# Two tiles to a transpose, the split behind it, and the update's first layer as one product in a graph network kernel

## The chip, the cores and the metric

The kernel runs on one core of a Trainium2 chip. A core has five engines that run side by side, each through its own instructions in order: TensorE (PE, with its weight loads listed as PEld), VectorE (DVE), ScalarE (ACT), GpSimd (POOL) and SyncE (SP), which here issues most DMAs. TensorE writes to PSUM, of which a bank holds 128 partitions of 512 float32. The metric is device time in microseconds (us); the median of nine runs before the change is 902.21 us (900.59 to 903.66).

## The reference: what is computed

There are 6250 nodes with 64 features and 206250 directed edges (100000 random pairs both ways, and a loop for each node), sorted by destination. Cut to what matters:

```python
h = max(layernorm(x), 0)
# first network: two graph convolutions
g = relu(relu((h + sum_of_neighbours(h)) @ W1 + b1) @ W2 + b2)
x = x + relu((g + sum_of_neighbours(g)) @ W3 + b3) @ W4 + b4
# second network: messages, their sum, update
h = max(layernorm(x), 0)
y = mlp3(h; WM1, WM2, WM3)                 # 64 -> 128 -> 128 -> 64, relu between
z = segment_sum(y[src], dst)
out = x + mlp3(concat([h, z]); WU1, WU2, WU3)   # 128 -> 128 -> 128 -> 64
```

All of it is float32. The sum over neighbours is taken as a product with a dense matrix of edge counts.

## The kernel before

**Tiles and layouts.** The nodes are 49 tiles of 128 (`NT`). "By node" is a tile with nodes on the partitions and features along the row; "by feature" has features on the partitions and up to four tiles of nodes (512 columns) along the row. The layers (`layer`, L444) want by feature, and a last layer (`last`, L453) gives by node back, one small product per tile.

**Precision.** Plain float32 products (FP) and float32r products (FR) are both used. A float32r operand is exact enough when the value is split into a rounded half and the rest (`halves`, L251: ACT copies with rounding, DVE subtracts). The product then runs over both halves.

**Build (to about 380 us).** For each of the 49 tiles a strip of the count matrix A is built from the edge list by one-hot products (L419), written to DRAM by SP (L425), and used at once for the first convolution (L569). Layers of that convolution run between, group by group. The halves of three weights are taken when the second strip is done (L611, L612): `w1p`, `m1p` and `u1p`. All weights are loaded at the start by SP's queue, ahead of the first store of A. A weight made with `twice` (L120) is loaded into both halves of the partitions, by two DMAs.

**Two sweeps (`sweep`, L693).** Each goes over 13 groups of up to four destination tiles (`GROUPS`: eleven of 4, one of 3, one of 2). A group takes 13 pieces of up to four source tiles. For a piece, SP loads counts as bytes (five buffers `a`), ACT or DVE widens them to float32r (L710, six buffers `ar`; pieces 1, 3, 6, 8 and 11 are ACT's), and TensorE multiplies into the group's sum `acc` (L717, two banks). The first sweep has two products per source tile (both halves of `h2r`), the second has one: its stationary operand is 64 columns of the rounded half of y beside 64 of the rest, so the sum of messages comes as two parts, on partitions 0 to 63 and 64 to 127.

**Behind each group** come the layers, `conv2` (L664) in the first sweep and `conv3` (L680) in the second. They are written one group late, behind the end of the next group's sum. A scheduler then places each instruction in its engine's queue, so the layers' products stand among the sweep's. The last groups of the first sweep reach into the second, which therefore leaves the last two pieces of its first two groups to the end of these.

`conv2` takes the group's sum through W3 and W4 (`ps_y` from w4), adds to x (`xs`), normalises to `h` (`norm`, L225), and calls `by_feature` (L438): `vr` gets both halves of h side by side, each tile is turned by its own transpose over 128 columns (L432, into bank `tf`), and ACT copies the bank to `h3f` (L435), which now holds the rounded half on partitions 0 to 63 and the rest on 64 to 127. Two products with `m1p` (the halves of the doubled WM1) give the message's first layer, one with `m2` the second, four small ones with `m3` the last; the result is split into `yr`.

`conv3` copies the sum to `f2` (`plain`, L659), and makes the update's first layer of three products into one bank: two float32r ones of `h3f` (kept for all nodes) with `u1p`, and a float32 one of `f2` with `u1z`, which holds the lower half of WU1 twice and so adds the sum's two parts:

```python
z = plain(acc, n, "f2")
t1 = layer(w.e1, n, "t1", *((part, h3f[:, columns(t, n)]) for part in u1p), (w.u1z, z))
```

Two more layers and the output's DMA follow.

Of the kernel before, what the change touches and what calls it, by code (L numbers as in the profile page):

```python
# [31 lines left out]
FP = mybir.dt.float32  # L32
# [5 lines left out]
FR = mybir.dt.float32r  # L38
AF = mybir.ActivationFunctionType
OP = mybir.AluOpType  # L40
AX = mybir.AxisListType

P = 128
N = 6250
E = 206250
D = 64
HID = 128
NT = (N + P - 1) // P
ROWS = NT * P
# [3 lines left out]
CH = 512  # L53
# [44 lines left out]
class Params:  # L98


    def __init__(self, nc, const, W1, b1, W2, b2, W3, b3, W4, b4,
                 WM1, bM1, WM2, bM2, WM3, bM3, WU1, bU1, WU2, bU2, WU3, bU3):
        self.loads = []

        def weight(w, name):
            t = const.tile(list(w.shape), FP, name=name)
            self.loads.append((t, w))
            return t

        def column(b, name):  # L110
            t = const.tile([b.shape[0], 1], FP, name=name)
            self.loads.append((t, b.rearrange("(f o) -> f o", o=1)))
            return t

        def row(b, name):
            t = const.tile([P, b.shape[0]], FP, name=name)
            self.loads.append((t, b.rearrange("(o f) -> o f", o=1).broadcast_to([P, b.shape[0]])))
            return t

        def twice(w, name):  # L120

            t = const.tile([P, HID], FP, name=name)
            self.loads += [(t[:D], w), (t[D:], w)]
            return t

        self.w1x, self.m1x, self.u1x = twice(W1, "w1x"), twice(WM1, "m1x"), twice(WU1[:D], "u1x")
        self.w1, self.w2, self.w3, self.w4 = self.w1x[:D], weight(W2, "w2"), weight(W3, "w3"), weight(W4, "w4")
        self.m1, self.m2, self.m3 = self.m1x[:D], weight(WM2, "m2"), weight(WM3, "m3")
        self.u1, self.u2, self.u3 = weight(WU1, "u1"), weight(WU2, "u2"), weight(WU3, "u3")
        self.c1, self.c2, self.c3, self.r4 = column(b1, "c1"), column(b2, "c2"), column(b3, "c3"), row(b4, "r4")  # L130
        self.d1, self.d2, self.s3 = column(bM1, "d1"), column(bM2, "d2"), row(bM3, "s3")
        self.u1z = twice(WU1[D:], "u1z")
        self.e1, self.e2, self.q3 = column(bU1, "e1"), column(bU2, "e2"), row(bU3, "q3")
        self.eps = const.tile([P, 1], FP, name="eps")
        nc.vector.memset(self.eps, EPS)
        self.ident = const.tile([P, P], FP, name="ident")
        make_identity(nc, self.ident)
# [15 lines left out]
def fast(ctx: ExitStack, tc: tile.TileContext, x, src, dst, w, bad, out):  # L153

    nc = tc.nc
# [7 lines left out]
    work = building.enter_context(tc.tile_pool(name="f_work", bufs=2))  # L163
# [3 lines left out]
    def bank(name, dtype=FP):  # L167
        return pmix.tile([P, CH * 4 // mybir.dt.size(dtype)], dtype, tag="mix", name=name)
# [38 lines left out]
    ps = bank("ps_smp")  # L207
# [43 lines left out]
    def halves(parts, v):  # L251

        first = nc.scalar.copy(parts[:, :, 0, :], v)
        nc.vector.tensor_tensor(parts[:, :, 1, :], v, parts[:, :, 0, :], op=OP.subtract)  # L254
        return first

    def weight_halves(w, name, pool=const):

        t = pool.tile([P, 1, 2, HID], FR, name=name)
        follow(halves(t, w[:, None, :]), "ACT")  # L260
        return [t[:, 0, i, :] for i in range(2)]
# [20 lines left out]
    def follow(op, engine):  # L282

        if engine in counted:
            behind(op, counted[engine])
# [25 lines left out]
    def search_block(b, i):  # L311

        if b >= len(BATCHES):
            return
        q = starts[b] + i
        blk = blks.pop(q)
        junk2 = wins.tile([P, BLK], BF, name="junk2", bufs=1)
        op = nc.scalar.activation(junk2, blk, AF.Sign, bias=below_node[:, q:q + 1], accum_out=sign2[:, q:q + 1])  # L318
        follow(op, "ACT")
        return op  # L320
# [104 lines left out]
        nc.sync.dma_start(A[t], a.rearrange("p h g -> p (h g)").bitcast(U8))  # L425
        return a

    def turned(vr, n, scale=1.0, to=None):

        ps = bank("tf")  # L430
        for j in range(n):
            nc.tensor.transpose(ps[:, j * P:(j + 1) * P], vr[:, j].rearrange("p i d -> p (i d)").bitcast(FP), w.ident)  # L432
        if to is None:
            to = work.tile([P, CH], FR, name="f1")[:, :n * P]
        nc.scalar.activation(to, ps[:, :n * P], AF.Copy, scale=scale)  # L435
        return to

    def by_feature(v, n, to):  # L438

        vr = work.tile([P, 4, 2, D], FR, name="vr")[:, :n]  # L440
        halves(vr, v)
        return turned(vr, n, to=to)

    def layer(bias, n, name, *terms):  # L444

        ps = bank("ps_" + name)
        for i, (wt, rhs) in enumerate(terms):
            nc.tensor.matmul(ps[:, :n * P], wt, rhs, start=(i == 0), stop=(i == len(terms) - 1))  # L448
        to = work.tile([P, CH], FP, name=name)[:, :n * P]
        nc.scalar.activation(to, ps[:, :n * P], AF.Relu, bias=bias)  # L450
        return to
# [9 lines left out]
    vr1, f1, t1s, t2s = {}, {}, {}, {}  # L461
# [83 lines left out]
    for i in range(2):  # L545
        op = search_block(1, i)
# [42 lines left out]
    for t in range(NT + 1):  # L589
        last_total, total = total, FirstSum(t - 1, a) if t else None  # L590
        if t < NT:
            def between(i):
                if total:
                    total.quarter(i)
                if last_total and i == 2:
                    last_total.check()
                for what, args in beside.get(4 * t + i, ()):
                    what(*args)

            a = build(t, between)  # L600
            if t == 0:
                values(5 * XT)
                for i in range(2):
                    search_block(2, i)
                fetch_edges(2)
                values(6 * XT)
                search(3)
                fetch_blocks(3)
                search(4)
            if t == 1:  # L610
                w1p = weight_halves(w.w1x, "w1p", once)  # L611
                m1p, u1p = weight_halves(w.m1x, "m1p"), weight_halves(w.u1x, "u1p")  # L612
        else:
            last_total.check()
            for i in range(4):
                total.quarter(i)
            total.check()
    m = MIXED
# [6 lines left out]
    late = ctx.enter_context(tc.tile_pool(name="f_late", bufs=1))  # L625
    work = ctx.enter_context(tc.tile_pool(name="f_work2", bufs=2))
# [1 line left out]
    wide = ctx.enter_context(tc.tile_pool(name="f_wide", bufs=6))  # L628
    pmix = ctx.enter_context(tc.tile_pool(name="f_pmix2", bufs=4, space=bass.MemoryType.PSUM))
    yr = late.tile([P, NT, 2, D], FR, name="yr")  # L630
    h3f = late.tile([P, ROWS], FR, name="h3f")


    stats = const.tile([P, 3], FP, name="stats")
# [6 lines left out]
    ps = bank("ps_stats")  # L641
# [14 lines left out]
    def columns(t, n):  # L656
        return slice(t * P, (t + n) * P)

    def plain(acc, n, name):  # L659
        to = work.tile([P, CH], FP, name=name)[:, :n * P]  # L660
        nc.scalar.copy(to, acc[:, :n * P])
        return to

    def conv2(t, n, acc):  # L664
        t1 = work.tile([P, CH], FP, name="t1")[:, :n * P]
        nc.scalar.activation(t1, acc[:, :n * P], AF.Relu, bias=w.c3)
        y = last(w.w4, t1, n)
        nc.vector.tensor_tensor(xs[:, t:t + n, :], xs[:, t:t + n, :], y, op=OP.add)
        h = work.tile([P, 4, D], FP, name="h")[:, :n, :]
        norm(h, t, n)  # L670
        nc.vector.tensor_tensor(xs[:, t:t + n, :], xs[:, t:t + n, :], w.q3[:, None, :].to_broadcast([P, n, D]), op=OP.add)
        f = by_feature(h, n, to=h3f[:, columns(t, n)])
        t1 = layer(w.d1, n, "t1", *((part, f) for part in m1p))
        t2 = layer(w.d2, n, "t2", (w.m2, t1))
        y = last(w.m3, t2, n)
        ys = work.tile([P, 4, D], FP, name="ys")[:, :n, :]
        nc.vector.tensor_tensor(ys, y, w.s3[:, None, :].to_broadcast([P, n, D]), op=OP.add)
        halves(yr[:, t:t + n], ys)

    def conv3(t, n, acc):  # L680
        z = plain(acc, n, "f2")
        t1 = layer(w.e1, n, "t1", *((part, h3f[:, columns(t, n)]) for part in u1p), (w.u1z, z))
        t2 = layer(w.e2, n, "t2", (w.u2, t1))
        y = last(w.u3, t2, n)
        o = work.tile([P, 4, D], FP, name="o")[:, :n, :]
        nc.vector.tensor_tensor(o, xs[:, t:t + n, :], y, op=OP.add)
        for t0, k, m in ((t, n, P),) if (t + n) * P <= N else ((t, n - 1, P), (t + n - 1, 1, N - (t + n - 1) * P)):
            if k:
                queue = nc.sync if m == P else nc.scalar
                queue.dma_start(out[ds(t0 * P, (k - 1) * P + m)].rearrange("(t p) d -> p t d", p=m),  # L690
                                o[:m, t0 - t:t0 - t + k, :])
# [294 lines left out]
```

## Time and profile before

| what | value |
|---|---|
| median of nine runs | 902.21 us (900.59 to 903.66) |
| profiled execution | 901.35 us, span 899.6 us |
| busy: PE, PEld | 848.3 (94%), 730.2 (81%) |
| busy: DVE, ACT, POOL | 621.8 (69%), 558.9 (62%), 117.9 (13%) |
| chain that ended last | PE 85%, DVE 6%, DMA 4%, ACT 2% |
| granted TensorE clock | 0.994 (mean) |
| transposes of both layers, L432 | 98, 15.2 us busy, mean 276 ns |
| update's first layer with u1p, L448 | 26, 7.9 us busy, mean 385 ns |
| update's first layer with u1z, L448 | 26 records for 13 products, 12.9 us busy, mean 576 ns |
| widening, L710 | DVE 220.4 us, ACT 234.4 us busy |

Busy times of TensorE's instructions overlap each other, since matmuls are pipelined; the chain of work that ended last gives what a piece of work takes of the time in a row of others. A float32 product is two records, a float32r product one.

### The profile page before, as it was taken

What the parts mean: (1) busy time and instruction counts of PE and PEld (TensorE: products, weight loads), DVE (VectorE), ACT (ScalarE), POOL (GpSimd) and SP (SyncE); (2) the same over time, 40 slices, a digit from 0 to 9 for tenths busy, and PEclk for the clock granted to TensorE, in tenths of its full rate; (3) what the DMA queues carried; (4) which work ended last, traced back from release to release, by engine and by line L of the source; (5) the groups of instructions that cost most, each with busy time, mean ns of one, the idle gap of its engine ahead of it and who ended that gap; (6) DMA issues with size and microseconds to landing.
All of it is one profiled execution on the core that took longest, in us unless ns stands there. A gap on an engine that the chain in (4) does not pass through costs nothing.

```text
span 899.6 us, 19658 instructions
## 1 busy us (share of the span) xinstructions
PE 848.3 (94%) x8248; PEld 730.2 (81%) x8248; DVE 621.8 (69%) x927; ACT 558.9 (62%) x744; POOL 117.9 (13%) x86
## 2 busy tenths in 40 slices
PE   0479999999999999999999999999999999999996
PEld 0369999999999999888777887777789767777785
DVE  6989999999999998544554544455545756666652
ACT  5556777777777666744445444545445787777763
POOL 3265533324421200000000000000000000000000
PEclk9989999999999999999999999999999999999999
DMA  6235444345433323745454444444434768888872
GB/s 149 75 135 185 149 148 149 146 147 181 147 142 149 121 109 146 202 113 142 118 132 120 124 126 119 117 119 127 122 93 115 203 175 231 221 240 221 236 185 66
DMA packets 195670, 133.70 MB, mean 149 GB/s; under 512 B 35220, under 2 KB 186900, under 8 KB 195572
## 3 DMA queue, kind: packets, MB, share of 16 engines
q1 hardware_dynamic: 189128, 121.32, 45.8%
q0 software_dynamic: 3600, 10.32, 4.0%
q8 instruction: 66, 1.08, 0.5%
q10 hardware_dynamic: 2844, 0.72, 0.4%
q14 instruction: 32, 0.26, 0.1%
HBM read 91.38 MB, written 40.94 MB: 147 GB/s over the span
## 4 chain that ended last, share of the span: by engine, by line
PE 85%; DVE 6%; DMA 4%; ACT 2%; issue 1%; POOL 0%; SPq 0%; ACTq 0%; DVEq 0%; POOLq 0%
PE acc L717 43%; PE acc L569 20%; PE cnt L419 8%; PE ps_t L448 7%; PE ps_y L457 4%; DMA a<-A 2%; DVE low L403 2%; ACT ar L710 1%; PE ps_g L487 1%; PE tf L432 1%; DMA blk<-in_dst_dram,row 1%; DVE high L400 1%; DVE there L396 1%; DMA d_win<-in_dst_dram,off 1%; DMA xs<-in_x_dram 1%
## 5 line engine op out<-in xcount | busy, mean ns | idle before, releaser
L710 DVE CAST ar<-a 128x2048 fp32r<-128x2048 uint8 (+2 forms) x208 | 220.4, 1072 | 200.5 <-PE acc L717 158.4
L710 ACT CAST ar<-a 128x2048 fp32r<-128x2048 uint8 (+2 forms) x130 | 234.4, 1805 | 137.4 <-PE acc L717 107.1
L717 PE MATMUL acc<-ar,h2r 128*128 128x512 f32 (+2 forms) x1274 | 297.1, 388 | 0.0
L717 PEld LDWEIGHTS acc<-ar,h2r 128*128 128x128 f32 x1274 | 229.8, 188 | 49.7 <-issue 5.7
L569 PE MATMUL acc<-hp,a 128*128 128x193 bf16 x2401 | 239.3, 249 | 4.7 <-ACT a L421 2.4
L421 ACT ACTIVATE a<-cnt 128x784 int16<-128x784 f32 x196 | 161.0, 823 | 81.3 <-PE cnt L419 80.5
L569 PEld LDWEIGHTS <-a 128*128 128x128 fp8e4 x2401 | 199.1, 99 | 6.7 <-ACT a L421 2.9
L717 PE MATMUL acc<-ar,yr 128*128 128x512 f32 (+2 forms) x637 | 158.3, 399 | 0.5 <-DVE yr L254 0.5
L717 PEld LDWEIGHTS acc<-ar,yr 128*128 128x128 f32 x637 | 115.4, 188 | 33.0 <-issue 10.3
L419 PE MATMUL cnt<-high,low 128*128 128x49 bf16 x3136 | 113.8, 186 | 15.6 <-DVE low L403 12.9
L419 PEld LDWEIGHTS <-low 128*128 128x128 fp8e4 x3136 | 106.8, 96 | 23.2 <-DVE low L403 13.9
L403 DVE TENSOR_TENSOR low<-there,lkw 128x2048 int32<-128x2048 bf16 (+2 forms) x51 | 112.2, 2200 | 0.0
L400 DVE TENSOR_TENSOR high<-high,lkw 128x3136 bf16<-128x3136 bf16 (+2 forms) x51 | 87.8, 1722 | 15.0 <-PE cnt L419 14.6
L307 POOL DMA_INDIRECT blk<-in_dst_dram,row x25 | 53.8, 2153 | 90.3 <-DVE base L299 78.1
L396 DVE TENSOR_TENSOR there<-word,lkw 128x2048 bf16<-128x2048 bf16 (+2 forms) x51 | 59.1, 1176 | 0.0
L332 POOL DMA_INDIRECT d_win<-in_dst_dram,off x25 | 27.1, 1084 | 83.1 <-DVE pair L355 44.0
L332 POOL DMA_INDIRECT s_win<-in_src_dram,off x25 | 34.7, 1389 | 7.6 <-issue 7.6
L450 ACT ACTIVATE t<-ps_t,d 128x512 f32<-128x512 f32 (+2 forms) x26 | 17.4, 668 | 11.6 <-PE ps_t L448 11.6
L385 PE MATMUL ps_win<-identb,parts 128*128 128x128 bf16 x75 | 8.9, 225 | 15.6 <-ACT parts L377 15.6
L450 ACT ACTIVATE t<-ps_t,c 128x512 f32<-128x512 f32 (+1 forms) x26 | 17.1, 663 | 7.8 <-PE ps_t L448 7.8
L450 ACT ACTIVATE t<-ps_t,e 128x512 f32<-128x512 f32 (+2 forms) x26 | 17.2, 663 | 5.3 <-PE ps_t L448 5.2
L318 ACT ACTIVATE junk<-blk,below_node 128x550 bf16<-128x550 int32 x25 | 18.7, 746 | 2.7 <-DMA blk<-in_dst_dram,row 2.5
(123 smaller groups left out, 578.0 us busy)
## 6 DMA issues: line engine op xcount, KB each, us to landing
a<-A SPq DMA_DIRECT2D x264, 256.0 KB, 3.1
A<-a SPq DMA_DIRECT2D x49, 784.0 KB, 3.8
a<-A SPq DMA_DIRECT2D x24, 192.0 KB, 2.5
a<-A SPq DMA_DIRECT2D x24, 128.0 KB, 2.2
a<-A SPq DMA_DIRECT2D x22, 64.0 KB, 2.2
out_dram<-o SPq DMA_DIRECT2D x11, 128.0 KB, 3.2
xs<-in_x_dram ACTq DMA_DIRECT2D x3, 224.0 KB, 5.7
xs<-in_x_dram SPq DMA_DIRECT2D x3, 224.0 KB, 6.2
```

The source lines that it names most:

```text
L307: nc.gpsimd.indirect_dma_start(out=blks[q], out_offset=None, in_=dst.rearrange("(r b) -> r b", b=BLK), in_offset=bass.IndirectOffsetOnAxis ...
L332: nc.gpsimd.indirect_dma_start(out=win[:, i, :], out_offset=None, in_=of.rearrange("(a o) -> a o", o=1), in_offset=bass.IndirectOffsetOnAx ...
L396: nc.vector.tensor_tensor(there, word2[:, None, :, :].to_broadcast(shape), of(0)[:, :, None, :].to_broadcast(shape), op=OP.is_equal)
L400: nc.vector.tensor_tensor(high, high2[:, None, :, :].to_broadcast(shape), of(1)[:, :, None, :].to_broadcast(shape), op=OP.is_equal)
L403: counted["DVE"] = nc.vector.tensor_tensor(low.rearrange("p (g i) w -> p g i w", i=2), there.rearrange("p g w i -> p g i w"), of(2)[:, :, ...
L419: counted["PE"] = nc.tensor.matmul(ps[:, b, j * H:(j + 1) * H], low[:, g, :], high[:, g // 2, :, g % 2], start=True, stop=True)
L421: counted["ACT"] = nc.scalar.activation(a[:, :, k:k + 2 * PG].rearrange("p h (b j) -> p h b j", b=2), ps[:, :, :PG * H].rearrange("p b (j ...
L448: nc.tensor.matmul(ps[:, :n * P], wt, rhs, start=(i == 0), stop=(i == len(terms) - 1))
L450: nc.scalar.activation(to, ps[:, :n * P], AF.Relu, bias=bias)
L569: nc.tensor.matmul(acc[:, t % 2, :], self.a[:, k, :], hp[:, k], start=(k == 0), stop=False)
L710: widen(ar.rearrange(f"p k t b -> {order}"), a.rearrange(f"p t (k b) -> {order}", b=P))
L717: nc.tensor.matmul(acc[:, :n * P], part, ar[:, k - k0].rearrange("p t b -> p (t b)"), start=(k == 0 and i == 0), stop=(k == H - 1 and i == ...
```

## The change

Three things change together. In `conv2`, `by_feature` is replaced by `features`: it turns h itself, two tiles to one transpose (64 features of one tile and 64 of the next on the 128 partitions), and splits what stands in the bank. For the even tiles ACT copies partitions 0 to 63 with rounding into `f`, and DVE subtracts that from the bank into the other 64 partitions of `f`; for the odd tiles it is the other way round. Since the message's first weight is there twice, either order of the halves gives the same product. ACT copies the bank a second time, unrounded, to partitions 0 to 63 of `hz`, where the tiles stand in their order again.

In `conv3` the sum's two parts are added by DVE (after ACT has copied one of them) into partitions 64 to 127 of `hz`, which then holds h and z, and the first layer is one float32 product with the whole of WU1.

So `u1x` and `u1z`, their four loads, `u1p` and its two operations are gone. `turned` loses the arguments that no one uses.

```diff
-        self.w1x, self.m1x, self.u1x = twice(W1, "w1x"), twice(WM1, "m1x"), twice(WU1[:D], "u1x")
+        self.w1x, self.m1x = twice(W1, "w1x"), twice(WM1, "m1x")
...
-        self.u1z = twice(WU1[D:], "u1z")
...
-    def by_feature(v, n, to):
-
-        vr = work.tile([P, 4, 2, D], FR, name="vr")[:, :n]
-        halves(vr, v)
-        return turned(vr, n, to=to)
...
-                m1p, u1p = weight_halves(w.m1x, "m1p"), weight_halves(w.u1x, "u1p")
+                m1p = weight_halves(w.m1x, "m1p")
...
-    h3f = late.tile([P, ROWS], FR, name="h3f")
+    hz = late.tile([P, ROWS], FP, name="hz")
...
-    def plain(acc, n, name):
-        to = work.tile([P, CH], FP, name=name)[:, :n * P]
-        nc.scalar.copy(to, acc[:, :n * P])
-        return to
+    def features(h, t, n):
+
+
+        ps = bank("tf").rearrange("p (i c) -> p i c", c=P)
+        for i in range(0, n, 2):
+            m = min(2, n - i)
+            nc.tensor.transpose(ps[:m * D, i // 2, :], h[:, i:i + m, :].rearrange("p t d -> p (t d)"), w.ident)
+        f = work.tile([P, 2, 2, P], FR, name="f1")
+        to = hz[:, columns(t, n)].rearrange("p (j c) -> p j c", c=P)
+        sides = [(slice(s * D, (s + 1) * D), slice((1 - s) * D, (2 - s) * D), s, (n + 1 - s) // 2) for s in range(2)]
+        for rows, _, s, k in sides:
+            nc.scalar.copy(f[rows, :k, s, :], ps[rows, :k, :])
+        for rows, others, s, k in sides:
+            nc.vector.tensor_tensor(f[others, :k, s, :], ps[rows, :k, :], f[rows, :k, s, :], op=OP.subtract)
+        for rows, _, s, k in sides:
+            nc.scalar.copy(to[:D, s::2, :], ps[rows, :k, :])
+        return f.rearrange("p i s c -> p (i s c)")[:, :n * P]
...
-        f = by_feature(h, n, to=h3f[:, columns(t, n)])
+        f = features(h, t, n)
...
-        z = plain(acc, n, "f2")
-        t1 = layer(w.e1, n, "t1", *((part, h3f[:, columns(t, n)]) for part in u1p), (w.u1z, z))
+        z = work.tile([P, CH], FP, name="f2")[D:, :n * P]
+        nc.scalar.copy(z, acc[:D, :n * P])
+        nc.vector.tensor_tensor(hz[D:, columns(t, n)], acc[D:, :n * P], z, op=OP.add)
+        t1 = layer(w.e1, n, "t1", (w.u1, hz[:, columns(t, n)]))
```

In the instruction order that the scheduler makes of it, the first sweep's group has its two transposes 26 sweep products behind `ps_y` of w4, then 16 sweep products, two with `m1p`, 4, `m2`, 4, `m3`, 48 (before: 40, four transposes, 4, `m1p`, 4, `m2`, 9, `m3`, 41). In the second sweep it is `u1`, 5 sweep products, `u2`, 7, `u3`, 37 (before: `u1p` twice, `u1z`, 4, `u2`, 8, `u3`, 37).

More of the change, by code (lines that the diff above doesn't have):

```diff
@@ L426, in build, with turned @@
         return a
-    def turned(vr, n, scale=1.0, to=None):
+    def turned(vr, n, scale):
         ps = bank("tf")
@@ L432, in turned @@
             nc.tensor.transpose(ps[:, j * P:(j + 1) * P], vr[:, j].rearrange("p i d -> p (i d)").bitcast(FP), w.ident)
-        if to is None:
-            to = work.tile([P, CH], FR, name="f1")[:, :n * P]
+        to = work.tile([P, CH], FR, name="f1")[:, :n * P]
         nc.scalar.activation(to, ps[:, :n * P], AF.Copy, scale=scale)
         return to
-    def by_feature(v, n, to):
-        vr = work.tile([P, 4, 2, D], FR, name="vr")[:, :n]
-        halves(vr, v)
-        return turned(vr, n, to=to)
     def layer(bias, n, name, *terms):
```

## The prediction

> **What bounds the kernel now.** I read the page's slices first, then the busy time by stage, then the chain of work that ended last, then the waits. The windows' columns are: stretch, its length, then busy time (and count) of PE, PEld, DVE, ACT, POOL, then the granted clock, DMA share and GB/s.
>
> ```profile
> 30.00:60.00 30.00, 18.47 (x274) 16.79 (x273) 29.15 (x61) 17.56 (x39) 12.51 (x9) 0.89 0.31 107
> 60.00:360.00 300.00, 297.00 (x5308) 288.73 (x5307) 280.92 (x362) 212.02 (x368) 90.42 (x57) 1.00 0.40 148
> ...
> 460.00:500.00 40.00, 40.00 (x185) 31.41 (x184) 18.55 (x30) 19.33 (x22) 0.00 (x0) 1.00 0.45 119
> ...
> 720.00:760.00 40.00, 38.37 (x165) 28.45 (x164) 24.27 (x31) 30.65 (x28) 0.00 (x0) 1.00 0.76 198
> ...
> 800.00:840.00 40.00, 40.00 (x171) 30.04 (x170) 26.12 (x25) 30.27 (x23) 0.00 (x0) 1.00 0.86 230
> ```
>
> The first sweep (380 to 703 us) and the second (703 to 894) are TensorE's: it has no gap except around 700 to 754, where the first sweep's last two groups meet the second. Elsewhere in the sweeps the widening engines wait for TensorE, not the reverse:
>
> ```profile
> DVE ar L710 <- PE acc L717: 151.4, 108, 4.5
> ACT ar L710 <- PE acc L717: 102.4, 66, 3.7
> ...
> ACT t L450 <- PE ps_t L448: 16.9, 21, 1.5
> ...
> DVE ar L710 <- DMA a<-A: 12.3, 17, 1.2
> ```
>
> So a product taken out of TensorE's queue there is worth what it takes of the chain, which is less than its mean duration, because neighbours overlap. The chain (start, length, what) has one turn of the first sweep and one of the second:
>
> ```profile
> 489.49 0.45 PE tf L432 x4
> 489.94 0.93 PE acc L717 x4
> 490.87 0.49 PE ps_t L448 x2
> 491.36 0.94 PE acc L717 x4
> 492.29 1.03 PE ps_t L448 x2
> ...
> 763.67 1.32 PE ps_t L448 x4
> 765.00 0.93 PE acc L717 x4
> 765.92 1.07 PE ps_t L448 x2
> 766.99 1.86 PE acc L717 x8
> 768.86 0.84 PE ps_y L457 x8
> ```
>
> The reader is to see prices: a transpose 0.45/4 = 0.1125 us, a 512-wide float32r product 0.93/4 = 0.233. Of the 1.32, the float32r pair with u1p is 0.47 and the float32 product with u1z the other 0.86.
>
> **The sum's base.** The profiled execution took 901.35 (span 899.6 and 1.75 around it), 0.86 below the median of nine, 902.21. I work out a difference and take it from the median.
>
> **Transposes (first sweep).** 49 become 25: 24 x 0.1125 = -2.70. No product takes their place. Bounds: -2.7, and 0 if TensorE stands where they were. The Trainium skill ("TensorE: Matmul & The Clock Gate", Part 4: PE-mode transpose) gives about 275 ns for one in a kernel and says that the full clock does not engage for them; the trace's mean in the sweeps is 279 ns, but four take 0.45 us of the chain at a granted clock of 1.00. By the page's figure this term would be 24 x 0.275 = -6.6 (an estimate), and the whole would end near 891.4; I stay with the chain.
>
> **The split behind the transposes.** Removed per group: ACT's vr copy 0.40 and h3f copy 0.60, DVE's vr subtraction 0.42. Added: four ACT copies (f, f, hz, hz) and two DVE subtractions, each of 64 partitions and 256 columns out of PSUM. Nearest rows: the 128x256 ops out of PSUM on DVE (L668, L677), 0.42, and ACT's 128x256 copies, 0.40. So ACT +0.6 and DVE +0.42 per group of 26.5 us, where they are busy 19 of 40 us. Bounds for one: 0.29 (row of 128x128) and 0.60 (row of 128x512). What counts is the wait it puts in TensorE's way: tf to m1p now passes an ACT copy and a DVE subtraction, each queued behind a widening. The new order gives that 14 to 16 sweep products of cover (3.3 to 3.7 us; 4 before) and puts tf 26 behind y of w4 (40 before). Laid on this turn of before:
>
> ```profile
> 485.30 0.42 DVE L239 SCALAR_TENSOR_TENSOR h<-xm,var 128x256 f32<-128x256 f32 x1
> 485.81 1.91 ACT L710 CAST ar<-a 128x2048 fp32r<-128x2048 uint8 x1 [1.43 <-PE acc L717]
> ...
> 487.66 1.23 DVE L710 CAST ar<-a 128x2048 fp32r<-128x2048 uint8 x1 [1.94 <-PE acc L717]
> ```
>
> tf would stand at 480.1 + 26 x 0.233 = 486.2, after h (485.72). ACT is free at 487.7, both f copies done at 488.5; DVE is through its widening at 488.9, both subtractions at 489.7; m1p is due at 486.2 + 0.22 + 16 x 0.233 = 490.15. Spare 0.45: cost 0. Behind the subtractions on DVE wait two widenings, ys and yr; TensorE has up to six widened buffers, 1.87 us each here, so it does not feel them. The hz copies end at 489.3, before t1's Relu needs ACT. If the cover failed: bound +1.1 per group (1.91 + 0.80 + 1.23 + 0.82 + 0.1 = 4.86 against 3.74).
>
> m2 to y of m3 has 4 products of cover where it had 9, but t2's Relu no longer stands behind a widening: m2 ends 493.32, Relu 0.70 to 494.1, weight load 0.19, y due at 494.25: short by 0.05 x 12 groups = +0.6. Bounds 0 and +2.2 (0.19 each, the whole weight load).
>
> The skill ("VectorE: DVE Perf Modes", Rules for kernel authors) would copy a matmul's output to SBUF first if many operations read it; here six read tf in PSUM. The rows show no dearer PSUM read (DVE 0.42 from PSUM, 0.42 from SBUF); such a copy would put 0.60 more per group into the cover, 0.15 over the 0.45 spare, 12 x 0.15 = +1.8 by that reading (an estimate).
>
> **The update's first layer (second sweep).** Per group u1p's two products go; the float32 product stays one (u1 over hz for u1z over f2, both 128 deep and 512 wide: 0.86). -0.467 x 10 full groups (1 to 10), -0.35 for the 384-wide: -5.0. Groups 0 and 12 come below. Bounds -5.0 and 0 (TensorE not the bound). DVE gets one add per group (64x512 out of PSUM; rows between L668's 0.42 and L254's h2r 0.69, I take 0.65, the same width), waiting for ACT's z copy (0.58, as before). It is issued a group early: between the widenings of pieces 5 and 7. Piece 5's widening starts when the sum g is complete; z is there 1.4 us after that, the add ends near 2.1, and piece 7's widening cannot begin before its buffer is free at 3.6 (0.86 + 2 x 0.93 + 0.86). Behind the add wait that widening and o: nothing late. DVE's 26 of 40 us becomes 28.
>
> **Between the sweeps.** Before, TensorE waits 2.3 us here (0.33, 0.71, 0.53, 0.52, 0.20). In the new order the last group's tf comes 28 products after y of w4, not 33 (-1.4 with the wait for vr gone). From tf to the end of group 0's first update layer it took 9.2 (726.10 to 735.3). Now: ACT's hz copies stand behind a widening that ends 4.0 after tf, t1's Relu ends 5.05, so m2 waits 1.35; y waits 0.57 (no cover); ys, yr and yr 1.0 as before; then group 0's sum, DVE's widening 1.23 ahead of the add, u1 at 9.8, done 10.7. +1.5 - 1.4: I take 0. Bounds -0.7 (the work removed: two transposes 0.22, a pair 0.47) and +2.6 (waits of 4.9 for 2.3).
>
> **Tail.** The last group's u1 waits for the copy and then the add: +0.46 (the 128x256 row 0.42 and a hop 0.04); its u1p pair was hidden behind the copy. Bounds +0.3 and +0.7.
>
> **Build.** u1p's halves go: ACT 0.30 and DVE 0.28. DVE is the bound there (29.15 of 30), so -0.28; bounds 0 and -0.3. Four loads of u1x and u1z leave SP's queue, ahead of the first store of A, which nothing waits for: 0. POOL's queue is unchanged.
>
> Sum: -2.70 + 0.6 - 5.0 + 0 + 0.46 - 0.28 = -6.9: **895.3**.
>
> **Rivals.**
> - *More than the sum (893.4).* u2 gets 5 products of cover, not 4. A full second-sweep turn takes 14.66 against 14.47 of priced work (49 x 0.233 + 0.47 + 2 x 0.86 + 0.84); the 0.19 could go too, -1.9 over ten groups. For it: TensorE's weight load waits for ACT's t in most turns. Against: y's cover shrinks from 8 to 7.
> - *The join costs (897.9).* The +2.6 above. For it: TensorE already waits there, DMA at 0.76. Against: tf is earlier.
> - *The second sweep is not TensorE's (900.3).* DMA moves 230 GB/s at 0.86 and five load buffers are few; then the -5.0 is lost, as it would be if u1 cost as much as u1p and u1z together. Against: widenings wait longer for TensorE than for loads, and single windows reach 264 GB/s.
> - *Slower: the split stalls TensorE in every group (908).* If subtraction follows both widenings at their worst, m1p waits 1.1 us in each of 12 groups, +13. It decides from 6.9/12 = 0.58 per group. For it: two engine hops behind 1.91 and 1.23 us widenings. Against: the reckoning above leaves 0.45 spare, and the buffers set the same phase in every group.
>
> **Numbers.** Chances: the sum 54%, more 11%, the join 14%, the second sweep 9%, the stall 12%. About 0.2% (1.8 us) is what can be told from no change; 900.3 is just at that edge, so I split its 9 into 3 faster and 6 same. Faster 54 + 11 + 14 + 3 = 82%, same 6%, slower 12%. The range 892.5 to 900.4 reaches from the first rival less 0.9 (half its gain again) to the third; it leaves the stall out.
>
> **What would show it.** In the new profile: 2 transposes and 0.22 us per turn of the first sweep and a turn near 26.3 (26.53 now); first-layer products of 0.86 in the second sweep and a turn near 14.2; no TensorE wait for f of DVE. Wrong would be: PE waiting for DVE's f in the first sweep, more than 3 us of idle TensorE between 695 and 750, or widenings waiting for loads in most turns after 750.

## The result, and the profile after

The changed kernel takes 907.03 us (median of 10 runs, 905.37 to 908.49) against 901.65 for the kernel before, run beside it (median of 31): a ratio of 1.0058, 95% interval 1.0050 to 1.0067. It is slower by about 5 us, where 7 us less were forecast. The profiled execution took 906.9 us (span 905.0; before 901.35 and 899.6), so the two traces show the same 5.4 us. Of all executions reported below one stands apart, at 2163 us (the split alone with six load buffers), and the ratio of that kernel leaves it out.

Four marks on TensorE divide them. A mark is the start of a group's last layer: of w4's products in the first sweep, of u3's in the second.

| stretch | before, us | after, us | difference | forecast |
|---|---|---|---|---|
| start to group 0 in the first sweep | 426.1 | 425.9 | -0.2 | -0.3 |
| group 0 to group 11, first sweep | 273.0 | 274.6 | +1.6 | -1.9 |
| from there to group 0 in the second sweep (the join) | 40.4 | 44.3 | +3.9 | -0.2 |
| group 0 to group 9, second sweep | 131.1 | 131.3 | +0.2 | -4.2 |
| from there to the end of the span | 29.0 | 28.9 | -0.1 | -0.4 |

(The forecast's terms are spread over the stretches by their number of groups: -0.225 and +0.05 per group in the first sweep, -0.467 in the second, the tail's +0.46 with the last groups.) Three stretches went wrong, and they are read in turn.

The windows of after, in three of the stretches shown of before (columns as there):

```profile
460.00:500.00 40.00, 40.00 (x180) 30.90 (x179) 19.39 (x32) 20.07 (x25) 0.00 (x0) 1.00 0.46 119
720.00:760.00 40.00, 35.50 (x140) 25.28 (x140) 24.51 (x36) 29.16 (x30) 0.00 (x0) 0.91 0.69 185
800.00:840.00 40.00, 38.84 (x168) 29.14 (x167) 27.49 (x28) 29.70 (x22) 0.00 (x0) 1.00 0.85 226
```

The first sweep looks unchanged. Around the join TensorE is busy 35.5 of 40 us and no longer 38.4, and its clock is 0.91. In the second sweep it is busy 38.84 of 40, where it had no gap.

**First sweep.** TensorE is full in both kernels, so the chain of waits has to tell. One turn of after, from the transposes to y (start, length, what):

```profile
513.40 0.34 PE tf L657 x2
513.73 3.27 PE acc L724 x14
517.00 0.66 PE ps_t L440 x2
...
520.55 0.96 PE ps_y L449 x8
```

Against the turn shown of before, two transposes take 0.34 for four at 0.45, m1p takes 0.66 for 0.49, and y of m3 0.96 for 0.85. Sum: -0.11 + 0.17 + 0.11 = +0.17, and the turn went from 26.54 to 26.70. None of the three is a pause that the busy share could show. Each is a weight load that comes late, as the timeline of an earlier turn shows for m1p:

```profile
487.95 1.23 DVE L717 CAST ar<-a 128x2048 fp32r<-128x2048 uint8 x1 [2.17 <-PE acc L724]
489.21 0.86 DVE L664 TENSOR_TENSOR f<-tf,f 64x256 fp32r<-64x256 f32 x2
...
490.18 0.30 PEld L440 LDWEIGHTS ps_t<-f,m1p 128*128 128x128 f32 x2 [0.37 <-issue]
490.21 0.70 PE L440 MATMUL ps_t<-f,m1p 128*128 128x512 f32 x2
```

The subtractions end at 490.07, the load starts at 490.18, and only then can the product run; a load that came 0.2 us earlier would have lain under the sweep's product before it. The profile names no releaser for this load ("issue"); that it waits for the subtractions is read from the times, and from before, where the loads of m1p, whose weights never change, wait for `h3f` (2.2 us in 10 waits between 420 and 690).

**Second sweep.** One turn of after:

```profile
766.11 1.91 ACT ar L717
...
768.08 1.90 ACT ar L717
...
770.01 0.58 ACT f L687
...
770.61 0.70 ACT t L442
...
771.35 1.13 PE ps_t L440 x2
```

Before, the shown turn of this chain ran through TensorE alone. Now it leaves TensorE: two widenings of ACT stand back to back, the copy of z behind them, then t1's Relu, and u2 waits for it. What the first layer saved on TensorE, TensorE then waits for ACT. Over 750 to 870 the chain that ended last lay on TensorE for 93% before, 5% on ACT and 3% on loads (DMA); after, for 59%, 25% and 12%. The sum of the widenings' waits for loads does not show this: 10.8 us before, 10.4 after.

**The join.** Windows of 2 us in after, where the last group's messages meet group 0's update:

```profile
736.00:738.00 2.00, 0.79 (x3) 0.35 (x2) 1.94 (x3) 1.98 (x2) 0.00 (x0) 0.51 0.01 2
738.00:740.00 2.00, 2.00 (x4) 0.87 (x4) 1.99 (x2) 1.19 (x3) 0.00 (x0) 0.50 0.66 167
740.00:742.00 2.00, 2.00 (x6) 1.61 (x5) 0.69 (x1) 0.98 (x2) 0.00 (x0) 0.50 1.02 285
742.00:744.00 2.00, 2.00 (x6) 1.08 (x5) 0.00 (x0) 2.00 (x2) 0.00 (x0) 0.78 0.24 71
```

The third number from the right is the granted clock: a half from 736 to nearly 743. Before, it is 1.00 there throughout, as in this row of before:

```profile
736.00:738.00 2.00, 2.00 (x8) 1.30 (x8) 1.04 (x1) 2.00 (x3) 0.00 (x0) 1.00 0.78 202
```

TensorE's waits in after between 700 and 750 (total, times, longest):

```profile
PE ps_t L440 <- ACT t L442: 1.5, 2, 1.1
PE ps_t L440 <- DVE hz L688: 1.2, 1, 1.2
PE acc L724 <- DVE yr L253: 1.0, 1, 1.0
PE ps_y L449 <- ACT t L442: 0.6, 1, 0.6
PE ps_t L440 <- DVE f L664: 0.3, 1, 0.3
```

They sum to 4.6 us, where before has 2.3. Behind them the work at half clock takes longer on the chain: u1 2.08 us (0.86 at full clock), five products of the sweep 2.13 (1.17), u2 1.42 (0.98 in the steady turn). That is 2.6 us of the join's 3.9.

### The profile page after: what moved, and what is told of

The parts are those of the page before. It is cut to its first block, busy times and chain, and to the rows that moved or that the text cites. A ratio compares the mean times of both kernels' runs of the same rounds, so it can differ in the third digit from the quotient of the medians.

```text
span 905.0 us, 19625 instructions
## 1 busy us (share of the span) xinstructions
PE 847.7 (94%) x8198; PEld 724.4 (80%) x8198; DVE 636.1 (70%) x952; ACT 566.3 (63%) x769; POOL 117.9 (13%) x86
## 4 chain that ended last, share of the span: by engine, by line
PE 80%; DVE 7%; DMA 5%; ACT 5%; issue 2%; POOL 1%; SPq 0%; ACTq 0%; DVEq 0%; POOLq 0%
PE acc L724 40%; PE acc L561 20%; PE cnt L418 8%; PE ps_t L440 6%; PE ps_y L449 4%; DMA a<-A 3%; ACT ar L717 3%; DVE low L402 1%; PE ps_g L479 1%; DVE high L399 1%; DMA blk<-in_dst_dram,row 1%; ACT t L442 1%; DVE there L395 1%; DMA d_win<-in_dst_dram,off 1%; DVE ar L717 1%
## 5 line engine op out<-in xcount | busy, mean ns | idle before, releaser
L682 DVE TENSOR_TENSOR ys<-ps_y,s 128x256 f32<-128x256 f32 (+2 forms) x13 | 5.3, 410 | 34.6 <-PE ps_y L449 34.6
```

## The experiments

The theory came to be this: the terms of the forecast were right as prices, but each gain was taken back by something that stood just behind it: weight loads in the first sweep, loads and ACT's queue in the second, TensorE's idle time and the clock at the join. Each expectation names its own theory A and the rivals to it.

A table of all kernels comes first, since three numbers of each trace (one trace for each kernel) are read again and again: the turn of the first sweep (mean of nine, groups 0 to 9), the join (from w4's products of group 11 to u3's of group 2, so with two turns of the second sweep in it) and the turn of the second sweep (mean of six, groups 2 to 8). The ratio is to the kernel before, run beside it. After and "join kept busy" share the code of the second sweep, and their turns there agree to 0.01.

| kernel | median us (before there) | ratio, 95% interval | first turn | join | second turn |
|---|---|---|---|---|---|
| before | 901.65 | 1 | 26.54 | 69.6 | 14.66 |
| after | 907.03 (901.65) | 1.0058 [1.0050, 1.0067] | 26.70 | 73.7 | 14.73 |
| split alone | 909.27 (901.58) | 1.0086 [1.0069, 1.0103] | 26.69 | 69.9 | 15.14 |
| update alone | 905.63 (901.58) | 1.0042 [1.0025, 1.0059] | 26.52 | 72.6 | 14.97 |
| sum's copy on DVE | 908.17 (901.58) | 1.0066 [1.0046, 1.0086] | 26.72 | 75.6 | 14.62 |
| join kept busy | 906.83 (901.58) | 1.0064 [1.0046, 1.0081] | 26.71 | 71.1 | 14.73 |
| after, third piece on DVE | 905.86 (901.65) | 1.0050 [1.0033, 1.0067] | 26.69 | 72.5 | 14.58 |
| after, six load buffers | 904.55 (901.65) | 1.0035 [1.0024, 1.0047] | 26.69 | 72.2 | 14.40 |
| before, third piece on DVE | 903.28 (901.65) | 1.0013 [1.0001, 1.0025] | 26.54 | 70.1 | 14.67 |
| after, third open sum, third piece on DVE | 899.27 (901.65) | 0.9977 [0.9966, 0.9988] | 26.72 | 66.6 | 14.62 |
| before, six load buffers | 901.11 (902.71) | 0.9983 [0.9973, 0.9992] | 26.54 | 67.7 | 14.59 |
| after, all three | 895.17 (902.71) | 0.9906 [0.9889, 0.9922] | 26.72 | 64.1 | 14.20 |
| before, all three | 913.56 (902.71) | 1.0134 [1.0098, 1.0171] | 26.55 | 70.0 | uneven |
| after, all three, more cover | 891.68 (902.71) | 0.9873 [0.9851, 0.9895] | 26.42 | 64.3 | 14.20 |
| before, six buffers, third piece on DVE | 927.77 (929.02) | 0.9986 [0.9960, 1.0012] | 26.54 | 67.3 | 14.60 |
| after, six buffers, third piece on DVE | 929.14 (929.02) | 0.9993 [0.9972, 1.0014] | 26.69 | 71.9 | 14.13 |
| split alone, six buffers | 931.30 (929.02) | 1.0014 [0.9987, 1.0042] | 26.68 | 69.8 | 14.67 |

The last three ran on a chip where every kernel, before too, takes some 27 us more. By the marks that is the build: group 0 of the first sweep comes at 453.9 to 455.9 in these three and near 426 elsewhere. Their totals have wide intervals, and they were made for their turns.

### One part of the change at a time

The transposes and the split alone, into before; the update stays in three products. `features` is that of the change, except that `f` is the group's columns of `h3f` and nothing is copied into `hz`:

```diff
-        f = by_feature(h, n, to=h3f[:, columns(t, n)])
+        f = features(h, t, n)
```

> Only the transposes of two tiles and the split behind them are taken from the change; the update's first layer stays in three products (its two float32r ones read the halves as they now lie), and h is not copied a second time. Theory A (each part loses at its own place: the split shows m1p and m3's products in the first sweep, the update's part makes the join wait): the first sweep's turn is 26.65 as after, its end 1.0 to 1.4 us later than before; the join loses less than half of the 2.9 us it lost after, with the granted clock at 1.00; the second sweep's turn stays 14.66. About 903 to 904.5 against 901.65 before. Rival B (the split is free and the whole loss is the update's): 900 or less, a turn of 26.3.

And the update's part alone, in which each tile is split and turned as before (`vr` with one buffer) and `hz` gets only the rounded half of h:

```diff
-        f = features(h, t, n)
+        vr = work.tile([P, 4, 2, D], FR, name="vr", bufs=1)[:, :n]
+        halves(vr, h)
...
+        nc.scalar.copy(f, ps[:, :n * P])
+        nc.scalar.copy(hz[:D, columns(t, n)], ps[:D, :n * P])
```

> Only the update's first layer is changed (one float32 product, sum added by DVE); transposes and split are as before, with one more ACT copy (64x512) of the rounded half of h for the update. The low half of h is left out of the update. Theory A: the first sweep is as before (turn 26.5), the join waits longer before the first product of the update and may fall to half clock (+1 to +4), the second sweep's turn is 14.7 as after, not 14.2, because ACT's queue (widening, widening, copy of the sum, Relu) releases the second layer: 903 to 906. Rival B (the gain of the update's part is real and the split alone eats it): a turn of 14.2, 896 to 898.

The first sweep's loss belongs to the split: its turn is 26.69 with it alone and 26.52 without it. It does not come from the copies into `hz`, which that kernel does not have. The join's loss belongs to the update: 69.9 with the split alone, 72.6 with the update alone, and there the clock falls in the same way:

```profile
734.00:736.00 2.00, 1.06 (x3) 0.34 (x3) 1.94 (x3) 1.98 (x2) 0.00 (x0) 0.50 0.00 0
736.00:738.00 2.00, 2.00 (x3) 0.91 (x4) 2.00 (x2) 1.21 (x3) 0.00 (x0) 0.50 0.62 162
```

Not expected: the split alone is the slower of the two, through a second sweep whose code is that of before (15.14 a turn). Its first sweep also starts 2.4 us later. In 750 to 870 its widenings wait 15.3 us (DVE) and 5.7 us (ACT) for loads, against 8.5 and 2.3 in before. This pointed to the loads.

### ACT's queue or the loads?

First the copy of z from ACT to DVE, to shorten ACT's path:

```diff
-        nc.scalar.copy(z, acc[:D, :n * P])
+        nc.vector.tensor_copy(z, acc[:D, :n * P])
```

> The changed kernel, with the copy of the sum's one part made by DVE instead of ACT. Theory A (second sweep bound by ACT's queue: two widenings of 1.9, the copy 0.58, the Relu 0.69, then the second layer): the Relu comes 0.5 earlier, TensorE's wait before u2 goes, a turn of 14.3 to 14.4, 902 to 904 against 907.0. Rival C (loads or DVE bound the second sweep): the turn stays at 14.7, or grows with DVE's longer queue; 907 or more.

The turn fell by only 0.1, to 14.62, and the join became worse (75.6; u1 waits 2.8 us for the add there, and the clock stays at a half until 745): the expected 14.3 to 14.4 was missed. u2's weight load waits 2.5 us for t in 750 to 870 where it had 6.0, but y's waits 5.2 where it had 1.8. So ACT's copy was not the whole of it. The next three take the two suspects one by one, with a control:

```diff
-            widen = nc.scalar.copy if c % 5 in (1, 3) else nc.vector.tensor_copy
+            widen = nc.scalar.copy if c % 5 in (1, 3) and not (late and c == 3) else nc.vector.tensor_copy
```

> The changed kernel with one thing moved: in the second sweep DVE, not ScalarE, widens the third piece of each sum, so that ScalarE has three widenings a turn there and the copy z, both Relus' chain and u2 no longer stand behind two widenings in a row. Theory A (the 0.47 us taken from TensorE's turn is lost because ScalarE's queue, 1.91 + 1.90 + 0.58 + 0.70, ends at the same point): the steady turn of the second sweep falls from 14.57 to 14.2-14.3 us, 10 turns, so 903-904 in all; TensorE's wait for t before u2 falls from 4.6 to under 2 us. Rival B (the loads set the turn: 3.3 us to landing, five buffers): the turn stays at 14.5-14.6, waits of the widening engines for DMA grow, 906-908. Rival C (DVE becomes the bound, it then has 26 + 3 of 40 us busy): the turn grows, over 908.

```diff
-    narrow = ctx.enter_context(tc.tile_pool(name="f_narrow", bufs=5))
+    narrow = ctx.enter_context(tc.tile_pool(name="f_narrow", bufs=6))
```

> The changed kernel with six load buffers of A instead of five, nothing else. Theory A (ScalarE's queue sets the second sweep's turn): the widenings' waits for DMA fall, the turn stays at 14.5-14.6 us, 906-908. Rival B (the loads set the turn): the turn falls to 14.2-14.3, 903-904.

> The kernel before with the same move as in the run above (third piece's widening to DVE in the second sweep): the control. Theory A: there ScalarE's path and TensorE's own work of 14.47 tie, so the turn falls only to TensorE's work, 14.66 to about 14.5: -1 to -2 us, 900-901. Rival B (loads): no change, 901.6. If it gains as much as the changed kernel does by the same move, the update's single product is worth nothing even with ScalarE out of the way.

Moving the piece gave 0.15 of a turn, six load buffers 0.33, and the move in before nothing (14.67). Neither suspect alone is the answer: theory A of these runs, ACT's queue, would have had 14.2 to 14.3 from the move, and the loads the same from the sixth buffer. The waits of the run with six buffers in 750 to 870 hold no line for a load any more, and loads have gone from its chain there, while 19% of it is still ACT's. Its longest waits:

```profile
DVE ar L717 <- PE acc L724: 29.0, 42, 1.1
ACT ar L717 <- PE acc L724: 26.6, 26, 1.8
...
PEld ps_t L440 <- ACT t L442: 4.6, 8, 0.6
```

What TensorE's own waits in that list name is ACT again: u2's load still waits for t. So both were to be taken away together, in both kernels. Before has no room for a sixth load buffer (the change freed it); its `vr`, used once in 26 us, gives up one of its two buffers for it.

> The kernel before with six load buffers, the control for the run of the changed kernel with six (904.55, its second sweep's turn 14.33). To make room the second layer's vr has one buffer in place of two; it is used once in 26 us. Theory A (before, TensorE's own 14.47 us of work nearly fills the turn, so loads and ScalarE could take away only 0.1-0.2): the turn goes from 14.6 to 14.5, -1 to -2 us, 900-901. Rival B (the loads alone set the turn in both kernels): the turn falls to 14.3 here too, about 899, and the single product is worth nothing.

> The kernel before with six load buffers (vr with one) and the third piece's widening on DVE in the second sweep, so that neither loads nor ScalarE's queue can hold it. Theory A (TensorE's own work is 14.47-14.5 a turn there): the turn 14.5-14.6, 899.5-901.5 in all. Rival B (loads and ScalarE together held this kernel too, as much as the changed one): 14.2-14.3, under 898, and the single product is worth nothing.

> The changed kernel with the same two moves and nothing else. Theory A: the turn 14.2, as the sum of the prediction had it, so 0.3-0.4 per turn or 3-4 us over ten groups below the kernel before with the same moves, in the second sweep; first sweep (+1.3) and join (+3 to +5) as in the changed kernel, 902-904 in all. Rival B: the turn 14.4 as with six buffers alone, 904-905.

Before stays at 14.59 and 14.60. After comes to 14.13. The chain of each now runs through TensorE alone; first before with both moves, from the first layer to u2:

```profile
849.71 1.33 PE ps_t L448 x4
851.03 0.93 PE acc L717 x4
851.96 0.98 PE ps_t L448 x2
```

and after with both:

```profile
854.10 0.86 PE ps_t L440 x2
854.96 0.93 PE acc L724 x4
855.88 0.98 PE ps_t L440 x2
```

The first layer is 0.86 for 1.33, and the turns differ by 0.47. The single product was worth its price, and it was hidden by loads and ACT together. Over ten groups that is the 4.7 us of the forecast. The totals of these two kernels still cannot be told from each other, as the first sweep and the join stay (+0.15 per turn, +4.6).

The same sixth buffer in the split alone:

> The transposes and the split alone, as in the first run, with six load buffers. That run lost 3-4 us in the second sweep, whose code is that of before. Theory A (its widenings waited for loads): the turn falls from 14.97 to 14.6 and the time from 909.3 to 904-906. Rival B (not the loads): stays at 908-910.

Its turn falls from 15.14 to 14.67: the slow second sweep was loads arriving late. Why the same code with five buffers waits longer for them there than in before is not settled. The total has an interval of half a per cent and says nothing.

### The join

Fourteen small float32 products that nothing uses stand in TensorE's queue where it waited: four behind m1p, two behind m2, four behind y, four ahead of u1.

```diff
+    def warm(n, after):
+        for i in range(n):
+            after = behind(nc.tensor.matmul(idle[:, :P], w.w2, w.w3, start=True, stop=True), after)
+        return after
```

> The changed kernel, with 14 small float32 products (128 columns, 0.21 us each) of constant weights into an unused bank, placed in TensorE's four waits of the join (4, 2, 4 and 4 of them). Theory A (the idle 5 us of the join lower the granted clock to a half for some 6 us, which costs 2.5): the clock stays 1.00, the first update product takes 0.86 to 1.1 of the chain, not 2.08; 904 to 905 against 907.0. Rival D (the products behind the join were late for their operands, not for the clock): no faster, up to 1 us slower.

The clock stays at 1.00 (compare the same windows of after above), and the join is 2.6 us shorter (71.1 for 73.7):

```profile
736.00:738.00 2.00, 1.83 (x12) 1.47 (x11) 1.69 (x2) 1.46 (x2) 0.00 (x0) 1.00 0.00 0
738.00:740.00 2.00, 1.71 (x6) 1.10 (x7) 1.97 (x3) 1.95 (x3) 0.00 (x0) 1.00 0.48 131
```

In the trace the span is 1.5 us shorter than after's. The ratios to before, 1.0064 [1.0046, 1.0081] and 1.0058 [1.0050, 1.0067], do not show it, so as a gain in time this run is inconclusive. That keeping TensorE busy keeps the clock is shown.

Work that is of use does the same. At the start of the second sweep a third group's sum is opened, in two PSUM banks that the build used and the sweeps leave empty, so TensorE does some 50 more products of the second sweep before group 0's u1 (152 records for 102; the expectation counts 24, and gives the banks to the turned messages):

```diff
+                if late and g % 4 > 1:
+                    accs[g] = spare.tile([P, CH], FP, tag="mix", name="acc")
...
-            order[:2 * pieces] = sorted(order[:2 * pieces], key=lambda x: (x[1] >= pieces - 2, x))
+            order[:3 * pieces] = sorted(order[:3 * pieces], key=lambda x: (x[1] >= pieces - 2, x))
```

> The changed kernel with DVE widening the third piece as above, and a third and fourth open sum at the start of the second sweep (in the two PSUM banks that the turned messages no longer use), so that TensorE has 24 more products to do between the last group's messages and the first update. Theory A (the join costs by TensorE's idle time and by the half clock that follows it): granted clock 1.00 between 733 and 745, the first update's end comes 3-5 us earlier against the rest of the work, 897-900 in all. Rival B (the join is bound by loads and widenings, which the third sum needs as well): TensorE waits for widened pieces in their place, 902-904.

The clock stays at 1.00, the join falls from 72.5 (the run with the third piece on DVE alone) to 66.6, and the kernel is the first below before: 0.9977 [0.9966, 0.9988]. The total lies inside the expected 897 to 900. The gain, 6.6 us on one chip, is more than the 3 to 5 us expected at the first update. It is near what the join of after lost to waits (4.6) and the half clock (2.6), but how it divides between the two is not shown.

### All together, and a control that failed

> The changed kernel with six load buffers, the third piece on DVE and the third open sum at the join together. Theory A (loads and ScalarE's queue each held the second sweep, and the join is another cost): the turn falls to 14.15-14.3, the join stays as in the run with the third open sum, 895-897 in all. Rival B (with six buffers the third piece's move brings nothing more, DVE's queue now ends last): the turn 14.3-14.4, 897-898.

> The kernel before with the same three additions as in the run above (vr with one buffer). The difference between the two is what the change is worth when loads, ScalarE's queue and the join no longer hide it. Theory A: the second sweep's turn stays at TensorE's 14.45-14.5 here, so this kernel is 2-3 us slower there than the one above, but 1.5-3 us faster in the first sweep, and about equal in all (896-898). Rival B (the single product is worth its 0.47 per group in full and the join no longer tells them apart): 899-900, slower than the one above by 3 or more.

After with six buffers, the third piece on DVE and the third sum takes 895.17: 0.9906 [0.9889, 0.9922]; its second sweep turns in 14.20. Before with the same three takes 913.56, against all that was expected. Its chain says why:

```profile
812.17 1.34 PE ps_t L448 x4
...
813.54 0.70 ACT t L450
...
814.28 1.14 PE ps_t L448 x2
...
815.45 0.70 ACT t L450
...
816.18 1.10 PE ps_y L457 x8
817.29 11.48 PE acc L721 x49
828.77 1.33 PE ps_t L448 x4
```

In four of the eight groups 2 to 9 the scheduler put first layer, u2 and y in a row, with no product of the sweep between them, so TensorE waits for both Relus, and such turns take 16.6 us (812.17 to 828.77) or more. It is another order of TensorE's queue and no control for the change; the pair with two moves above is. So how much of the 895.17 before could have had from the same additions is not shown.

### More cover in the first sweep

On top of the 895.17 kernel, `conv2` is issued in steps, so that 22 products of the sweep stand between the transposes and m1p (14 to 16 before), 10 before m2 (4) and 6 before y of m3 (4); the copies into `hz` come last:

```diff
-        f = features(h, t, n)
+        f, keep = features(h, t, n)
+        yield
...
+        yield
         y = last(w.m3, t2, n)
+        keep()
...
+            if steps and g < end and c in (5, 7):
+                next(steps[0], None)
```

> As the run with six load buffers, third piece on DVE and third open sum, and in the first sweep the message's layers are issued in three steps, so that 22 products of the sweep stand between the transposes and m1p (16 before), 10 before m2 (4) and 6 before m3 (4), and the copies into hz are issued behind the last layer. Theory A (the first sweep lost its saved transposes because m1p and m3 waited 0.19 and 0.11 us, their cover too short): no wait for f or t, the turn falls from 26.7 to 26.3-26.4, 10 turns, -3 to -4 us against the run it is built on: 892-894. Rival B (the turn is set by something else, since e.g. the split alone took 26.7 with the same cover): the turn stays at 26.6-26.7, 895-898.

One turn of its chain:

```profile
485.47 0.22 PE tf L658 x2
485.69 5.11 PE acc L733 x22
490.81 0.46 PE ps_t L440 x2
491.27 2.33 PE acc L733 x10
493.59 1.04 PE ps_t L440 x2
494.64 1.39 PE acc L733 x6
496.02 0.84 PE ps_y L449 x8
```

m1p is back at 0.46 and y at 0.84, and the turn fell from 26.72 to 26.42, below before's 26.54. That is the 0.20 of m1p and the 0.12 of y. The transposes gained nothing by it: the turn shown is one of two in which they take 0.22, and in the others they still take 0.30 to 0.44, since the first one's weight load waits for h (3.1 us in 8 waits between 420 and 690). The kernel takes 891.68 us against 902.71: 0.9873 [0.9851, 0.9895], so it beats both. Theory A held in size: -3.5 for the -3 to -4 expected.

## Why the prediction was wrong, point by point

Result and forecast lie some 12 us apart: 3.5 in the first sweep, 4.1 in the join, 4.4 in the second sweep. Three of the prediction's four rivals name one of these places each. They were priced as alternatives, and all three places lost at once.

**Transposes, -2.70.** The price was right where h is there in time: two take 0.22 us of the chain in two turns of after, four took 0.45. In the other full turns they took 0.31 to 0.37, as the first transpose's weight load waited for h (2.7 us in 8 waits between 420 and 690); about half of the gain was gone there. The turn on which the prediction laid the new work, with h ready ahead of tf, is one of the two with 0.22: one turn was taken for all. The Trainium skill's 275 ns for each ("TensorE: Matmul & The Clock Gate", Part 4: PE-mode transpose) would have made the gain 0.55 a turn; no run here shows that on the chain.

**The split at no cost, because 0.45 us were spare at m1p: failed.** The step laid the new work on one turn of before and let m1p's product wait for the subtractions. Two things were missing. The widening ahead of the subtractions began at 487.95, not at 487.66, and they took 0.86, not 0.82, which left 0.17 of the 0.45: they end at 490.07, and m1p's product comes due at 490.24 in the chain of after. And m1p's weight load stands behind the same wait and needs 0.19 of its own ahead of the product. That 0.19 was counted at y of m3, one sentence on, and not at m1p. The rival that made the split a loss of 1.1 us per group was the right place at a sixth of the size: it was given as a stall by late widenings, and it is +0.17.

**y of m3, +0.6.** Measured +0.11 a turn, so +1.3 over 12 groups: the mechanism held, twice the size, inside the bound.

**The first layer, -5.0: the term was right as a price and failed as a gain.** 0.86 for 1.33 in every group, and nothing of it in the time. The step that failed is "The first sweep and the second are TensorE's" (the second was, in before, and ceased to be once its turn was to be shorter), and behind it the ground against the third rival, that widenings wait longer for TensorE than for loads. That rival (-5.0 lost, given 9%) is what happened. The sum of waits was the wrong evidence. An engine that feeds TensorE through a ring of buffers waits for it whenever the ring is full; how much shorter TensorE's turn may become before the ring is empty is another number. An estimate of it was there in the rows: a load needs 3.3 us to land and its buffer is then held for a widening of 1.23 (DVE) or 1.91 (ACT), 13 pieces (seven of 1.23, five of 1.91 and a last one of 0.43, on average 1.43) in five buffers: 13 x (3.3 + 1.43) / 5 = 12.3 us a turn with no piece ever waiting for its engine. By itself that would allow a turn of 14.2. But of 14.65 it leaves 2.35 x 5 / 13 = 0.9 us per piece for waiting, less than half of one ACT widening that stands in front. The other rival on this sweep, that 0.19 more could go because 14.66 holds only 14.47 of priced work, has no support either: with loads and ACT out of the way before keeps 14.60, and u2 takes 0.98 of its chain, where the sum counts 0.86.

**The second sweep's DVE add, hidden.** It was, in the steady turns: between 750 and 870 TensorE never waits for it. What stood in the way was ACT.

**Join 0, bounds -0.7 and +2.6: failed, outside its bound.** It cost +3.9. The waits became 4.6 for 2.3, nearly as the upper bound had it (4.9). The term that it put at nothing without a reason is what idle time on TensorE costs afterwards: 2.6 us at half clock. No row of before shows a half clock in the sweeps. The Trainium skill ("TensorE: Matmul & The Clock Gate", Part 1: The HAM clock gate) says that the clock is halved after an idle window of about 3.4 us. Here no single wait was longer than 1.2 us. TensorE was busy 1.80 us of the 3.4 before the clock fell (732.6 to 736.0), and 1.83 of 3.4 in the update alone (730.3 to 733.7). So the trace agrees with the halving, but it came without an idle window of that length. The share of idle time that brings it is not shown: the kernel before with the third piece on DVE was busy only 1.64 of 3.4 us (726.6 to 730.0) and kept 1.00.

**Tail and build.** -0.1 for -0.4 and -0.2 for -0.3: within what the marks can tell.

## What to carry to other kernels

Before pricing an instruction out of a full TensorE, work out what the next queue needs for a turn (how long a load takes to land and then waits behind the feeding engine's other work, for the loads in flight; each feeding engine's own chain up to the layer), and give the gain only down to that. A late operand costs a weight load as well as a wait, in every layer that lost its cover. And at a seam between two stages count TensorE's idle time as a whole, not wait by wait, since a sparse stretch can be paid a second time at half clock; here a further sum to work on there was worth more than the change itself.

## What the runs showed of the hardware that was not expected

- The clock fell to 0.50 though TensorE had been busy for half of the time before it (1.80 of 3.4 us, no wait over 1.2), and stayed there until nearly 743, though TensorE was fully busy from 738. In another kernel 1.64 of 3.4 us did not lower it.
- ACT's copies of the bank `tf` into `hz` waited for DVE's subtractions from the same bank (16.6 us in 10 waits in after's first sweep), though they need only what the transposes wrote. It did not lengthen the first sweep's turn (the split alone has no such copies, and 26.69); what orders the two readings was not tried.
- The second sweep of the split alone, with TensorE's instructions in the order of before, was half a microsecond a turn slower with five load buffers and within 0.1 of before with six.
